# A planned GNN layer: transfers with a distant due time wait while the transfer queue has a backlog

## The chip, the core and the metric

The kernel runs on one NeuronCore of a Trainium2 chip. A core has a TensorE (PE) for matrix products with a separate weight load (PEld), a VectorE (DVE), a ScalarE (ACT), a GpSimd (POOL) and a SyncE (SP). Each has its own queue of instructions and works through it in order; they meet through semaphores. SP only issues transfers (DMAs) here; GpSimd issues some as well. The metric is device time in microseconds (us) for one execution of the whole program; lower is better.

## The reference

One layer of a graph network on 64 graphs of 256 nodes with 256 channels, in fp32. `h` is the layer-normed input after a ReLU, and the layer adds a gated recurrent unit's output to x:

```python
h = jnp.maximum(_layernorm(x, axis=-1), 0.0)
# _L0_gnn_ref(h, adj): h is called x inside it
xc = jnp.transpose(x, (0, 2, 1))
h = relu(bn1(conv1d(xc, conv1_w)))              # 1 tap
h = bn2(conv1d(h, conv2_w, pad=8))              # 17 taps along the nodes
x_conv = jnp.transpose(relu(h + xc), (0, 2, 1))
s = x @ w_se.T + b_se                           # 3 numbers for each node
A = jnp.exp(-dist(s, s)) * mask                 # mask is the adjacency, 256x256 for each graph
x_nmp = einsum('bnm,bmd->bnd', A, relu(x @ w_msg.T + b_msg))
gi = concatenate([x_conv, x_nmp]) @ w_ih.T + b_ih
gh = x @ w_hh.T + b_hh
r, z = sigmoid(gi_r + gh_r), sigmoid(gi_z + gh_z)
out = x + (1 - z) * tanh(gi_n + r * gh_n) + z * x
```

Here `dist` is the squared distance of the two nodes' `s`, and the last line is cut down: inside the layer x means h, and the outer addition uses the layer's own input.

## The kernel before

**Work and loops.** Graphs are handled in pairs (i = 0 to 31) and four pairs make a block of eight graphs; there are eight blocks, called b0 to b7 here (the loop `for b in range(NB)`, line 1237). Inside a block, `nxt` is the first pair of the next one, so each block also prepares the next.

**The 17-tap convolution** is done in 16 frequency bins. `forward` splits the rows into the bins' operands U, V, PT and Sv on VectorE; `product` (line 879) multiplies a bin's operand with that bin's filter spectrum, in four 128x128 matmuls (eight rows in the trace, since an fp32 matmul leaves two). The text counts a block's 47 products as P1 to P47. The spectra lie in DRAM (`filt`): each is a 256 KB load by SP into one of nine slots `wb` (`load_kinds`, line 854). A product gives its slot back and the next load is issued, so the 47 loads W1 to W47 of a block are spread through its products. Two of the nine slots (tz0, tz1) come free only a few products into a block. `branch_back`, `odd_back`, `q_back`, `p_back` and `join` bring the products back on VectorE.

**The other steps of a block.** `message` (w_msg matmuls), `embed` (two transposes "ident,z" and copies to zT), `affinity` (nine-row matmuls of zT, then exp and the product with the adjacency on ACT and DVE, into e), `aggregate` (e,msg matmuls), `conv1` and `split` for the next block, and `gates`, whose matmuls are combined in seven products for each pair (`seven`).

**Transfers, which is what the change concerns.**
- `load_x` (line 591): x of a pair, two DMAs on SP.
- `turn_h` (763): ACT writes hh, then a DMA transpose on SP, written T:halves<-hh; `sort_h` (774): four DMAs hh<-halves on SP; `join_h` (781): ACT copies to hT.
- `turn_adj` (602): a DMA transpose of the adjacency on SP into `halves`, then halves_d<-halves to DRAM; `load_adj` (609): four DMAs adjh<-halves_d on GpSimd; `join_adj` (619): ACT copies.
- `finish` (1156): a DMA transpose of the output on SP (T:gn<-back), ACT copies to back, then on GpSimd two accumulating loads of x onto back and two writes to out. The finish of a block's last pair is done in the next block.
- In b0, GpSimd also loads the gate weights w_ih and w_hh, 2.3 MB.

**What sets the order.** Every engine call goes through `Recorder.record` (line 332), which makes a Task with a modelled cost and, for a transfer, a `size` in us of the transfer queue's service. All instructions therefore carry line 369, the call made there, in the profile. `plan` (line 383) is a list scheduler. It gives each tensor task a due time `late`, the sum of tensor costs ahead of it in program order, and passes due times back to what a task needs. It then takes, again and again, the engine that can begin soonest, and on it the ready task with the earliest due time:

```python
cand = [(max(free[e], at, lane if T[k].size else 0.0), T[k].late, k, at) for at, k in ready[e]]
if cand:
    now = min(cand)[0]
    best.append((now, min(c[1:] for c in cand if c[0] <= now + 1e-9), e))
```

`self.dma` is the modelled time at which all transfers issued so far are through; `lanes` allows eight in flight for SP (with ACT) and eight for GpSimd. `emit` (line 448) then issues the calls in the planned order; nothing is decided on the chip. There are three plans: a prologue in its written order (`emit(True)`), one for the first forward transform and the filter spectra, and one for all eight blocks.

Of the kernel before, what the change touches and what calls it, by code (L numbers as in the profile page):

```python
# [249 lines left out]
class Recorder:  # L250
# [8 lines left out]

    LANES = 8  # L260
    TURN = 1.9
    LAG = {"tensor": 0.25, "vector": 0.14, "scalar": 0.16, "gpsimd": 0.2, "sync": 0.0}
    OWN = {"tensor": 0.0, "vector": 0.12, "scalar": 0.12, "gpsimd": 0.1, "sync": 0.0}

    def __init__(self, nc):
        self.nc, self.tasks, self.live, self.masks = nc, [], {}, {}
        self.first, self.planned, self.dma = None, 0, 3.0
        self.lanes = [deque([0.0] * self.LANES) for _ in range(2)]
        self.free = dict.fromkeys(self.LAG, 0.0)
        for name in ("tensor", "vector", "scalar", "gpsimd", "sync"):  # L270
# [61 lines left out]
    def record(self, engine, op, args, kw):  # L332
# [7 lines left out]
        if op.startswith("dma"):  # L340
            if "transpose" in op:
                size, cost = 2.5, self.TURN
            elif "accum_op" in kw:
# [33 lines left out]
    def lag(self, u, v):  # L377
        return 0.0 if u.size else (self.OWN if u.engine == v.engine else self.LAG)[u.engine]

# [3 lines left out]
    def plan(self, fixed=False):  # L383

        T, new = self.tasks, range(self.planned, len(self.tasks))
        self.planned = len(T)
        total = 0.0
        for k in new:
            t = T[k]
            for p in t.preds:  # L390
                T[p].succs.append(k)
            if t.engine == "tensor":
                t.late = total
                total += t.cost
        for k in reversed(new):
            t = T[k]
            for s in t.succs:
                t.late = min(t.late, T[s].late - self.lag(t, T[s]) - self.cost(t))
            if t.first is not None:
                t.late = t.first - 1e6  # L400
        ready, free = {e: [] for e in self.LAG}, self.free
        left = {}

        def enable(k):
            at = max((T[p].done + self.lag(T[p], T[k]) for p in T[k].preds), default=0.0)
            ready[T[k].engine].append((at, k))
        for k in new:
            left[k] = sum(p in left for p in T[k].preds)
            if not left[k]:
                enable(k)  # L410
        order = []

        def commit(k, e, at, now):
            t = T[k]
            ready[e].remove((at, k))
            t.begin = now
            free[e] = t.done = now + t.cost
            if t.size:
                if t.cost == self.TURN:
                    free[e] = max(free[e], self.dma + 1.1)  # L420
                self.dma = max(self.dma, now + 1.6) + t.size
                t.done = self.dma + 1.1
                lanes = self.lanes[e == "gpsimd"]
                lanes.popleft()
                lanes.append(t.done)
            order.append(k)
            for s in t.succs:
                left[s] -= 1
                if not left[s]:
                    enable(s)  # L430
        while fixed and len(order) < len(new):
            k = new[len(order)]
            e = T[k].engine
            at = next(at for at, j in ready[e] if j == k)
            commit(k, e, at, max(free[e], at, self.lanes[e == "gpsimd"][0] if T[k].size else 0.0))
        while len(order) < len(new):
            best = []
            for e in ready:
                lane = self.lanes[e == "gpsimd"][0]
                cand = [(max(free[e], at, lane if T[k].size else 0.0), T[k].late, k, at) for at, k in ready[e]]  # L440
                if cand:
                    now = min(cand)[0]
                    best.append((now, min(c[1:] for c in cand if c[0] <= now + 1e-9), e))
            now, (_, k, at), e = min(best)
            commit(k, e, at, now)
        return order
# [972 lines left out]
```

## Time and profile before

| | |
|---|---|
| median of 10 runs | 1771.15 us (1763.25 to 1778.35) |
| profiled execution | 1774.74 us, its span 1773.0 us |
| TensorE busy | 1694.2 us (96%) |
| VectorE, ScalarE, GpSimd busy | 1465.9, 1035.6, 300.9 us |
| mean granted TensorE clock | 0.987 |
| share of the DMA engines busy, b2 to b6 | 0.61 to 0.68 in each block |
| first product of b0 to b7 | 109.8, 324.4, 531.85, 738.1, 948.5, 1152.7, 1360.6, 1565.9 us |

How to read it: busy times are of one profiled execution, and its span is the time from its first to its last instruction. In a timeline a row is a run of like instructions: the start in us, its length, the engine, the line, the operation, output and inputs by tile name, and how many; in brackets, how long the engine sat idle before it and who ended that. In the list of waits a row gives the waiting engine and tile, what ended the wait, and then us in total, how often, and the longest. "128x128" is partitions by elements of the tile.

### The profile page before, as it was taken

Reading aid. Unit: us, or ns where it says so; the run is one execution under the profiler, and the core shown is the slowest. Engines: PE = TensorE matmul, PEld = TensorE weight load, DVE = VectorE, ACT = ScalarE, POOL = GpSimd, SP = SyncE. Lnnn points to the kernel's source line nnn. Section 1 sums busy time; section 2 is a strip of 40 time slices with the busy share of each in tenths; the row PEclk is TensorE's granted clock in tenths of the full one; section 3 lists DMA queues with packets and bytes.
Section 4 is the critical chain, followed back from the end, with each engine's and each line's share of the span. In section 5 each row is a group of like instructions: output and inputs, shape, how many; then the busy total and the mean of one; then the engine's idle time right before and its main releaser. Section 6 shows DMA issues by size and latency. Waiting matters only on the chain.

```text
span 1773.0 us, 26175 instructions
## 1 busy us (share of the span) xinstructions
PE 1694.2 (96%) x8950; PEld 1427.4 (81%) x8950; DVE 1465.9 (83%) x3400; ACT 1035.6 (58%) x1949; POOL 300.9 (17%) x353
## 2 busy tenths in 40 slices
PE   5999999999999999899999999999999999999996
PEld 3678788888789778797888887897788978888885
DVE  4889798698897988878987988979888889869543
ACT  2554656665755756556665757557665666556443
POOL 2210222103210221102211132102211022110010
PEclk9999999999999999999999999999999999999998
DMA  7775565973569465693658835694656936383122
GB/s 189 238 242 169 107 131 120 214 207 84 114 133 280 110 126 112 172 250 84 120 119 217 199 90 114 135 272 118 126 112 176 252 78 119 74 232 130 18 55 48
DMA packets 319992, 260.94 MB, mean 147 GB/s; under 512 B 209096, under 2 KB 242148, under 8 KB 319859
## 3 DMA queue, kind: packets, MB, share of 16 engines
q1 hardware_dynamic: 278506, 199.04, 45.4%
q0 software_dynamic: 38400, 57.58, 15.6%
q10 hardware_dynamic: 2953, 2.66, 0.8%
q8 instruction: 70, 1.15, 0.3%
q14 instruction: 63, 0.52, 0.1%
HBM read 156.03 MB, written 43.78 MB: 113 GB/s over the span
## 4 chain that ended last, share of the span: by engine, by line
PE 76%; DVE 9%; ACT 4%; DMA 4%; issue 2%; POOL 2%; ACTq 0%; DVEq 0%; POOLq 0%
PE acc L369 51%; PE aux L369 25%; DMA wb<-filt 4%; DVE V L369 2%; DVE T L369 2%; DVE Yv L369 2%; ACT adj L369 1%; POOL rstd L369 1%; POOL shift L369 1%; DVE U L369 0%; DVE e L369 0%; ACT Yv L369 0%; DMA x<-in_x_dram 0%; ACT hh L369 0%; DVE acc L369 0%
## 5 line engine op out<-in xcount | busy, mean ns | idle before, releaser
L369 PE MATMUL acc<-wb,w_ih 128*128 128x256 f32 x768 | 192.4, 379 | 0.0
L369 PEld LDWEIGHTS acc<-wb,w_ih 128*128 128x128 f32 x768 | 145.9, 190 | 19.8
L369 POOL DMA_DIRECT2D adjh<-halves_d x112 | 66.6, 600 | 531.6 <-ACT adj L369 445.4
L369 PE MATMUL acc<-wb,w_x 128*128 128x256 f32 x576 | 138.0, 384 | 8.3 <-DVE acc L369 8.3
L369 PE MATMUL aux<-wb,w_x 128*128 128x256 f32 x576 | 141.5, 384 | 1.5 <-DVE wb L369 0.9
L369 DVE SCALAR_TENSOR_TENSOR V<-T,V 128x128 f32<-128x128 f32 (+2 forms) x448 | 140.8, 376 | 0.0
L369 PEld LDWEIGHTS acc<-wb,w_x 128*128 128x128 f32 x576 | 108.5, 191 | 35.9 <-DVE acc L369 14.1
L369 POOL TENSOR_TENSOR rstd<-rstd,neg_half 128x4 f32<-128x4 f32 x32 | 86.8, 2714 | 279.3 <-DVE shift L369 252.7
L369 PEld LDWEIGHTS aux<-wb,w_x 128*128 128x128 f32 x576 | 107.3, 191 | 22.1 <-DVE wb L369 3.7
L369 PE MATMUL aux<-w_msg,hT 128*128 128x259 f32 x512 | 124.4, 383 | 0.4 <-ACT fo L369 0.4
L369 PE MATMUL acc<-V,wb 128*128 128x128 f32 x1024 | 121.4, 276 | 1.4 <-DMA wb<-filt 1.3
L369 PEld LDWEIGHTS acc<-V,wb 128*128 128x128 f32 x1024 | 118.8, 192 | 4.0 <-DMA wb<-filt 1.8
L369 POOL DMA_DIRECT2D back<-in_x_dram x62 | 61.5, 1151 | 346.1 <-ACT back L369 346.1
L369 PEld LDWEIGHTS acc<-U,wb 128*128 128x128 f32 x1024 | 119.0, 195 | 1.3 <-issue 0.3
L369 PE MATMUL acc<-U,wb 128*128 128x128 f32 x1024 | 119.4, 278 | 0.0
L369 PE MATMUL acc<-hT,w_hh 128*128 128x256 f32 x384 | 106.2, 385 | 6.9 <-ACT acc L369 6.9
L369 PE MATMUL acc<-Yv,w_ih 128*128 128x256 f32 x384 | 110.6, 384 | 0.9 <-ACT Yv L369 0.8
L369 PE MATMUL aux<-hT,w_c 128*128 128x512 f32 x224 | 107.4, 596 | 3.7 <-ACT e L369 2.7
L369 ACT COPY back<-gn 128x1024 uint16<-128x1024 uint16 x62 | 79.7, 1338 | 53.2 <-DMA gn<-back 53.2
L369 ACT ACTIVATE gn<-acc,bn_columns 128x512 f32<-128x512 f32 x64 | 44.0, 687 | 113.4 <-PE acc L369 110.4
L369 PE MATMUL acc<-wb,w_hh 128*128 128x256 f32 x384 | 109.4, 380 | 0.0
L369 PE MATMUL aux<-e,msg 128*128 128x256 f32 x448 | 109.1, 381 | 0.0
(177 smaller groups left out, 3943.5 us busy)
## 6 DMA issues: line engine op xcount, KB each, us to landing
wb<-filt SPq DMA_DIRECT2D x376, 256.0 KB
back<-in_x_dram POOLq DMA_DIRECT2D x62, 256.0 KB, 7.6
out_dram<-back POOLq DMA_DIRECT2D x62, 256.0 KB, 4.3
x<-in_x_dram SPq DMA_DIRECT2D x58, 256.0 KB
halves_d<-halves SPq DMA_DIRECT2D x28, 512.0 KB
adjh<-halves_d POOLq DMA_DIRECT2D x112, 128.0 KB, 3.1
hh<-halves SPq DMA_DIRECT2D x108, 128.0 KB
filt<-fo POOLq DMA_DIRECT2D x18, 252.0 KB, 5.7
```

The source lines that it names most:

```text
L369: self.tasks.append(Task(engine, lambda: method(*args, **kw), cost, size, self.first))
```

## The change

`plan` gets a notion of how far TensorE's work has come in due times: `self.pace` is the largest `late` of the tensor tasks planned so far. A transfer whose own `late` is more than CALM = 20 us beyond that, and finite, isn't a candidate before `self.dma - 1.0`, that is until the modelled transfer queue is within 1 us of being empty. The candidate's time is now worked out by `when`. Transfers without a due time (the output's) and the fixed prologue are as before. All three plans are made with the new code.

```diff
     TURN = 1.9
+    CALM = 20.0
...
         order = []
+        self.pace = 0.0
+
+        def when(e, at, t):
+            now = max(free[e], at)
+            if t.size:
+                now = max(now, self.lanes[e == "gpsimd"][0])
+                if self.pace + self.CALM < t.late < math.inf:
+                    now = max(now, self.dma - 1.0)
+            return now
 
         def commit(k, e, at, now):
             t = T[k]
             ready[e].remove((at, k))
             t.begin = now
             free[e] = t.done = now + t.cost
+            if e == "tensor":
+                self.pace = max(self.pace, t.late)
             if t.size:
...
             for e in ready:
-                lane = self.lanes[e == "gpsimd"][0]
-                cand = [(max(free[e], at, lane if T[k].size else 0.0), T[k].late, k, at) for at, k in ready[e]]
+                cand = [(when(e, at, T[k]), T[k].late, k, at) for at, k in ready[e]]
```

## Prediction

> **What bounds the kernel now.** I read the page first: busy shares, then the chain that ended last.
>
> ```profile
> PE 1694.2 (96%) x8950; PEld 1427.4 (81%) x8950; DVE 1465.9 (83%) x3400; ACT 1035.6 (58%) x1949; POOL 300.9 (17%) x353
> ...
> PE 76%; DVE 9%; ACT 4%; DMA 4%; issue 2%; POOL 2%; ACTq 0%; DVEq 0%; POOLq 0%
> ```
>
> TensorE sets the end. Its idle time is 1773.0 − 1694.2 = 78.8 us, and a change of order can win only from this, or from time in which the PE runs slow. TensorE's waits say whose it is:
>
> ```profile
> PE aux L369 <- DMA bn_rows<-in_bn_v_dram: 15.5, 1, 15.5
> PE acc L369 <- DMA wb<-filt: 10.4, 12, 2.4
> PE acc L369 <- DVE acc L369: 8.3, 10, 1.9
> PE acc L369 <- ACT acc L369: 6.9, 7, 1.1
> ...
> PE aux L369 <- ACT zT L369: 4.3, 7, 1.6
> ```
>
> The first, before the loops, isn't touched. The second is what the rule can reach: 10.4 us in which a product waits for its filter. I placed each in TensorE's timeline. Three (0.64, 1.44, 2.38 us, 4.5 together) are the first products of b2, b3 and b6; most of the rest (5.9 us) falls on the 15th to 22nd product of a block, where the block's four 128 KB adjh transfers run beside the filter stream. That place in b4:
>
> ```profile
> 961.97 0.60 PE L369 MATMUL aux<-e,msg 128*128 128x256 f32 x2
> 962.93 1.16 PE L369 MATMUL acc<-Sv,wb 128*128 128x128 f32 x8 [0.37 <-DMA wb<-filt]
> 963.93 1.06 PE L369 MATMUL acc<-V,wb 128*128 128x128 f32 x8
> 964.82 1.03 PE L369 MATMUL aux<-e,msg 128*128 128x256 f32 x4
> ```
>
> A product is eight rows, 0.9 us. The planner puts aggregation matmuls (e,msg) and message matmuls (w_msg) between P15 and P24; they cover most of the lateness, and 0.37 us shows. Last, b6's start, in SP's, GpSimd's and TensorE's timelines:
>
> ```profile
> 1335.18 0.38 SPq L369 DMA_DIRECT2D halves_d<-halves  x1
> 1335.73 3.36 SPq L369 DMA_TRANSPOSE gn<-back  x1
> 1354.15 7.92 SPq L369 DMA_DIRECT2D wb<-filt  x8
> ```
> ```profile
> 1353.48 0.63 POOL L369 DMA_DIRECT2D out_dram<-back  x1 [2.55 <-DMA back<-in_x_dram]
> ```
> ```profile
> 1360.60 3.81 PE L369 MATMUL acc<-Sv,wb 128*128 128x128 f32 x32 [2.38 <-DMA wb<-filt]
> ```
>
> The block's last output write runs into W1, the block's first filter load: W1 lands 5.6 us after issue, and 2.8 us in b4, where that write was issued 2.9 us ahead of it and not 0.7.
>
> **What the Trainium skill says.** "DMA: Bandwidth & Descriptors", section "Issuing engines are not separate DMA queues": transfers issued by SP, ACT and GpSimd share the same 16 engines and interleave. The trace agrees: W17 of b4 took 4.9 us from issue to landing, W18 to W21, beside GpSimd's adjh, 5.9 to 7.5. So withholding SP's x or transposes doesn't remove the adjh burst. The same page, "Rules for kernel authors", row "Use all 16 engines": an outer dimension under 16 confines a transfer to that many engines. The trace agrees for x (outermost 8): 256 KB take about 2.0 us of the queue, a filter load of that size 0.67. "TensorE: Matmul & The Clock Gate", Part 1: after an idle window of about 3.4 us the clock is halved. The trace agrees: after a 1.57 us wait in b1 the clock records show half speed from 355.9 to 362.7 and the U products are stretched (8.50 us for 56 rows, 7.31 for 64 in b4).
>
> ```profile
> 354.53 2.86 PE L369 MATMUL aux<-zT 9*128 9x256 f32 x8 [1.57 <-ACT zT L369]
> 357.32 1.23 PE L369 MATMUL aux<-w_msg,hT 128*128 128x259 f32 x2
> 358.34 8.50 PE L369 MATMUL acc<-U,wb 128*128 128x128 f32 x56
> ```
>
> **The change part by part.** No instruction is added or removed; every engine gets the same ones in another order from b0 on. In b2 to b6, SP's order was W1–21, x, W22–24, T:halves<-hh, W25–33, hh, W34–35, hh, W36–41, two hh, T:gn, W42–47. It becomes W1–33, T:halves<-hh, W34–41, three hh, W42–47, hh, T:gn, then adjacency transpose and two x. TensorE's order, planned on these imagined landings, becomes P1–P24 without a break, eight e,msg matmuls together, P25–32, eight w_msg together, P33–40, then both ident,z transposes and four zT matmuls in one group.
>
> (a) *SP before W22.* One x (2.0 us of service) and one transpose (about 1.8 of service, SP held 7.7 us) leave the stream's first half. It matters only from W22 on: W16 to W21 were issued ahead of x in both kernels. Gain for P22–P24 about 2 us of landing.
>
> (b) *TensorE P16–P24 unfilled.* I replay b4 with its own landings: P(k) starts at the later of P(k−1)'s end and its filter. P16 is ready at 961.97 and needs W18 (W11 and W14 fill late slots, for P22 and P23), landed 962.89: 0.9 us. P18 and P19 wait 0.7 each for W20 and W21 (965.42, 967.00). With (a), P24 ends near 972.4; then 8 e,msg at 0.43 = 3.46 us, and the four w_msg matmuls already done by this point before, 1.73: 977.6, against 975.85 where P25 begins now: +1.75. The same for b2, b3, b5, b6: +1.4, −1.0 (its 2.23 us stall at P17 is part of the old time), +1.4, +1.9. If the burst is longer than before this grows one for one, since nothing is left to fill.
>
> (c) *zT merged.* The nine-row zT groups cost about 0.3 us of pipe entry each and a wait of 0.39 in b4; in one group, later: −0.6 a block. (b)+(c) for b2–b6: 0.8 − 1.6 + 1.2 + 0.9 + 1.4 = **+2.7**.
>
> (d) *b1.* The zT group moves behind P44, so the 1.57 us wait and the half-speed spell (products at twice 111 ns: about 3.8 us) go; its P1–P24 stretch costs +2 as in (b): **−3.3**.
>
> (e) *b7.* P1–P24 costs +1.3, but the planner moves T:gn from W21 to W41 and P24's followers start earlier; at 1627–1639 TensorE waits 0.62, 0.49 and 0.92 for DVE and ACT, then runs at half clock for about 6.8 us (3.4 lost), 5.4 in all. I take 60% of it as won: −3.3. **−2.0**, both ends +1.3 and −4.1.
>
> (f) *Block starts.* T:gn of the last finish is now ahead of halves_d. Before it waited for the adjacency transpose to land (1335.05 in b6) though ACT had written back by 1334.5, and shared the engines with halves_d (3.28 us); so it lands 1 to 3 us sooner, and the two back accumulations and the two output writes with it. W1's issue is tied to the last gate's slots and stays. Of the 4.5 us at block starts I take **−3.0**; bounds 0 and −6.2 (all of it, and 1.7 for the half-speed spell, 738.2 to 741.6, behind b3's). halves_d, now behind T:gn, is 3 to 4 us later; its adjh readers wait in a 25 us gap of GpSimd.
>
> (g) *b0.* W10–47 run without a break, but GpSimd puts one rstd power ahead of w_ih and w_hh (2.3 MB, 5.9 us of service at 0.67 us per 256 KB), so they start near 117 and not 110.3, beside W18 onward: 0 to +4 for P16–P24. DVE, the bound later in b0 (waits of 0.80, 0.73, 1.87 and 0.85 between 176 and 204), meets weight_sums (10 us) later: −2 to +3. I take **0**, bounds −2 and +6.
>
> (h) *Hidden moves.* hh×4, T:gn and x end up to 8 us later; the hT they feed is read near 1008 in b4 and landed near 994, x is needed near 1028. At least 6 us remain, so nothing; without that cover the price is the excess, one for one. GpSimd's shift power is now ahead of the first adjh: 0.2 us, inside the burst already priced. The T:halves<-hh behind W33 holds SP up to 7.7 us; the 3.46 us of w_msg behind P32 and seven full slots (7 × 0.9 = 6.3) cover it: nothing, at worst 1 us a block.
>
> Sum: 2.7 − 3.3 − 2.0 − 3.0 + 0 = −5.6. The profiled execution took 1774.74 us, span 1773.0 and 1.7 around it, 3.6 over the median of 1771.15; −5.6 on it gives a span of 1767.4, and on the median **1765.5**.
>
> **The rivals.**
>
> *Faster (0.45):* the sum, 1757 to 1765.8. Its support is the stalls with clock loss at 354 and 1627, which the new orders break up.
>
> *No change (0.28), about 1769.5:* stalls move rather than go. The transfers are hidden anyway, as b4's single 0.37 us stall suggests; (f) yields nothing because the out write still meets W1, and (d) only: 2.7 − 3.3 − 2.0 + 1 = −1.6.
>
> *Slower (0.27), about 1781:* P16–P24 unfilled. Its waits come as runs of 0.7 to 1 us over two or three products. In the trace waits of 1.44, 1.57 and 2.23 us were each followed by a half-speed spell, which costs 1.7 us for each 3.4 us of it; one of 2.38 was not. With the upper replay (+1.9) and that loss in five blocks: 5 × 3.6 = 18, −0.6 × 5 for zT, less (d)+(f) at half (−3), −2: about +10. It decides from roughly 1.4 us of idle in 3.4 us; b4's replay has 2.3 us over about 5 us, so it is near. Against it: b6 had 1.19 us at one product and no slow spell.
>
> **How the numbers follow.** Forecast 1765.5. Repeated runs scatter by 0.4% each way, and about 0.3% (5.3 us) is what a measurement can tell. Range 1755 to 1779: below it (e), (f) and (g) would all be at their best ends; above it lie the slower case's upper third. The likeliest case's own range is 1757 to 1765.8. Faster 0.45, same 0.28, slower 0.27.
>
> **What would show it.** Right: waits for wb still about 8 to 12 us, but in runs at P16–P21 and none at b3's and b6's first products; zT in b1 under 0.5 us and full clock at 355–363; fewer waits at 1627–1639. Wrong: slow-clock spells some 15 us into the blocks (slower), wb waits under 3 us in sum (the rule frees more than I think), b0's first product of b1 later than 324.4 by over 3 us (w_ih), or a long T:halves hold behind W33.

## The result, and the profile after

The changed kernel takes 1760.33 us (median of 14 runs, 1753.08 to 1768.03) against 1771.19 for the kernel before (49 runs). The ratio is 0.9938, 95% interval 0.9923 to 0.9953: 11 us faster. The forecast was 1765.5, with a range of 1755 to 1779 and 0.45 on faster. The profiled execution took 1753.68 us, its span is 1751.9; it is 6.7 below its median, and that of before was 3.6 above its own. The pair of profiles therefore shows 21 us where the runs show 11, so the sizes of stages below are taken over several profiles.

One sentence on the change has to be put right: most output transfers do have a due time, through the reuse of `back` by the next pair's gates. Only the last pair's have none. The rule reaches them too.

Busy shares and chain of the changed kernel (its instructions carry line 370, those of the experiments mostly 373):

```profile
PE 1669.7 (95%) x8950; PEld 1415.1 (81%) x8950; DVE 1463.5 (84%) x3400; ACT 1036.2 (59%) x1949; POOL 308.5 (18%) x353
...
PE 81%; DVE 7%; DMA 6%; ACT 2%; issue 2%; POOL 1%; SPq 0%; ACTq 0%; DVEq 0%
```

TensorE is still the bound. Its idle time has not shrunk (1751.9 − 1669.7 = 82.2 us, 78.8 before); its busy time has, by 24.5 us, with the same 8950 matmuls. So the gain is not in a smaller total of waits. TensorE's waits of the changed kernel agree:

```profile
PE acc L370 <- DMA wb<-filt: 13.0, 20, 1.5
PE acc L370 <- ACT acc L370: 10.3, 7, 1.7
...
PE aux L370 <- ACT zT L370: 2.1, 3, 0.8
```

The waits for filters grew from 10.4 us in 12 to 13.0 in 20, but the longest fell from 2.4 to 1.5; those for ACT's acc grew from 6.9 to 10.3; those for zT fell from 4.3 to 2.1. Busy time can fall in two ways. First, matmuls can run at half clock for less time: between the prologue and the last 20 us the clock records of before hold seven 3.41 us windows at half speed, those of after two (129.1 and 340.7 us), and a window costs about 1.7 us, half its length. That belongs to this pair of executions and not to the change: six profiles of kernels with the rule in b2 to b6, without the fillers of the experiments below, hold one to seven such windows (3.7 on average), the four with the old order two to seven (3.75). Five windows are 8.5 us, most of what the pair of profiles shows beyond the runs. Second, TensorE can spend less time on the nine-row zT groups, which counts as busy; that comes below.

P1 to P25 of b5, TensorE's timeline, changed kernel:

```profile
1139.33 3.81 PE L370 MATMUL acc<-Sv,wb 128*128 128x128 f32 x32 [0.54 <-ACT e L370]
1142.98 7.31 PE L370 MATMUL acc<-V,wb 128*128 128x128 f32 x64
1150.13 3.78 PE L370 MATMUL acc<-Sv,wb 128*128 128x128 f32 x32
1154.72 1.13 PE L370 MATMUL acc<-V,wb 128*128 128x128 f32 x8 [0.82 <-DMA wb<-filt]
1156.80 6.52 PE L370 MATMUL acc<-V,wb 128*128 128x128 f32 x56 [0.94 <-DMA wb<-filt]
1163.15 3.62 PE L370 MATMUL aux<-e,msg 128*128 128x256 f32 x16
```

It is the picture of the forecast's step (b): P1 to P24 bare, two waits beside the adjh burst, P24 finished 23.8 us after P1 (forecast 23.9), then e,msg in one piece. P1 waits 0.54 us for ACT, as it did in this block before. At the start of b6, where P1 waited 2.38 us for its filter, the same 0.54 us is now all that is left. The end of b5 shows why, in SP's, GpSimd's and TensorE's timelines:

```profile
1317.84 1.77 SPq L370 DMA_TRANSPOSE gn<-back  x1
1319.77 1.05 SPq L370 DMA_DIRECT2D halves_d<-halves  x1
1338.34 6.97 SPq L370 DMA_DIRECT2D wb<-filt  x9
```
```profile
1333.61 0.63 POOL L370 DMA_DIRECT2D out_dram<-back  x1 [1.44 <-DMA back<-in_x_dram]
```
```profile
1342.94 3.25 PE L370 MATMUL acc<-Sv,wb 128*128 128x128 f32 x27 [0.54 <-ACT e L370]
```

The last output write is issued 4.7 us ahead of W1, not 0.7.

Times from one block's first product to the next one's (b7: to the start of TensorE's last instruction), from five profiles; the edits of the last two are described below:

| block | before | changed | changed, again | before + tail swap | changed + hh behind acc |
|---|---|---|---|---|---|
| b0 | 214.7 | 213.1 | 216.8 | 213.7 | 212.1 |
| b1 | 207.4 | 205.2 | 206.4 | 207.4 | 203.9 |
| b2 | 206.3 | 203.8 | 205.7 | 206.7 | 203.3 |
| b3 | 210.4 | 203.8 | 204.2 | 205.8 | 202.9 |
| b4 | 204.2 | 203.5 | 204.1 | 206.8 | 202.8 |
| b5 | 207.9 | 203.6 | 208.4 | 205.4 | 203.5 |
| b6 | 205.3 | 204.2 | 204.2 | 205.0 | 202.7 |
| b7 | 199.7 | 197.4 | 201.2 | 197.1 | 196.9 |

b4, on which the forecast was worked out, is the best of the steady blocks of before: the others spread up to 6 us above it.

### The profile page after: what moved, and what is told of

Its sections match the earlier page's. It is cut to its first block, busy times and chain, and to the rows that moved or that the text cites. A ratio compares the mean times of both kernels' runs of the same rounds, so it can differ in the third digit from the quotient of the medians.

```text
span 1751.9 us, 26185 instructions
## 1 busy us (share of the span) xinstructions
PE 1669.7 (95%) x8950; PEld 1415.1 (81%) x8950; DVE 1463.5 (84%) x3400; ACT 1036.2 (59%) x1949; POOL 308.5 (18%) x353
## 3 DMA queue, kind: packets, MB, share of 16 engines
q8 instruction: 70, 1.15, 0.3%
## 4 chain that ended last, share of the span: by engine, by line
PE 81%; DVE 7%; DMA 6%; ACT 2%; issue 2%; POOL 1%; SPq 0%; ACTq 0%; DVEq 0%
PE acc L370 55%; PE aux L370 26%; DMA wb<-filt 4%; DVE V L370 2%; DVE T L370 1%; DVE e L370 1%; DVE acc L370 1%; DMA x<-in_x_dram 1%; DVE U L370 1%; DMA T<-in_x_dram 1%; POOL shift L370 1%; DVE st L370 0%; DMA halves<-hh 0%; DVE tr L370 0%; ACT gn L370 0%
## 5 line engine op out<-in xcount | busy, mean ns | idle before, releaser
L370 POOL TENSOR_TENSOR rstd<-rstd,neg_half 128x4 f32<-128x4 f32 x32 | 91.7, 2867 | 285.0 <-DVE shift L370 257.0
L370 PE MATMUL acc<-hT,w_hh 128*128 128x256 f32 x384 | 105.6, 382 | 10.3 <-ACT acc L370 10.3
L370 DVE TENSOR_TENSOR T<-Yv 128x512 f32<-128x512 f32 (+1 forms) x80 | 42.5, 581 | 87.0 <-ACT Yv L370 86.4
L370 PEld LDWEIGHTS aux<-w_msg,hT 128*128 128x128 f32 x512 | 96.3, 190 | 15.1 <-ACT fo L370 0.8
L370 DVE TENSOR_TENSOR acc<-acc,wb 128x512 f32<-128x512 f32 x64 | 44.2, 691 | 72.2 <-PE acc L370 71.6
```

The lines of the kernel that those rows point to most:

```text
L370: self.tasks.append(Task(engine, lambda: method(*args, **kw), cost, size, self.first))
```

## The experiments

**Early and late half.** The rule is switched by how far TensorE's due times have come; b2 begins at 397 us of them. The early half holds in b0 and b1 only, the late half from b2 on; SP's orders are in each block exactly those of one kernel or the other.

```diff
-                if self.pace + self.CALM < t.late < math.inf:
+                if self.pace + self.CALM < t.late < math.inf and self.pace < 395.0:     # early; late: >= 395.0
```

> The rule applies in b0 and b1 only; from b2 on the orders are those of the kernel before. Theory of the forecast (parts d and g): b1 loses its 1.57 us wait for zT and the half-speed spell behind it, b0 gains nothing: about -3 us, ratio 0.998. Rival 'steady blocks': everything comes from b2 to b7, ratio 1.000 (within 0.001). Rival 'b0 and b1 hold most of it': below 0.996.

> The complement: the rule applies from b2 on only, b0 and b1 are those of the kernel before. Theory of the forecast: about -2.3 us (+2.7 for b2 to b6, -3.0 at block starts, -2.0 in b7), ratio 0.9987. Rival 'steady blocks': -8 to -11 us, ratio 0.994 to 0.9955.

Measured: early 1768.38 us, ratio 0.9972 (0.9955 to 0.9989); late 1759.42 (five runs), ratio 0.9919 (0.9900 to 0.9938), the kernel before beside them 1773.56. The early half is as forecast. The late half is not −2.3 us but some −14 (interval −11 to −18), so the steady blocks hold most of the gain. The two add to some −19 us, more than the −11 of the whole; only the ends of the intervals meet. Whether the late half alone is better than the whole is therefore open.

**The tail swap alone.** From here on a kernel makes both plans, with and without the rule, and edits one engine's order before it is issued.

```diff
 # SP, ends of b0 to b5, orders of the kernel before
  T:halves<-in_adj
- halves_d<-halves
  T:gn<-back
+ halves_d<-halves
  W1 ...
```

> The kernel before with one edit: at the ends of b0 to b5 the last T:gn<-back is issued ahead of halves_d<-halves instead of behind it. Theory of the block starts (part f): the waits of the first products for wb in b2, b3 and b6 go, and with them the half-speed spell behind b3's: -3 to -6 us, ratio 0.9965 to 0.998. Rival 'the products' own order wins': no change, ratio 0.9995 to 1.0005.

Measured: 1766.22 us, ratio 0.9962 (0.9944 to 0.9979). TensorE at the start of b6 in this kernel:

```profile
1354.58 3.59 PE L373 MATMUL acc<-Sv,wb 128*128 128x128 f32 x30 [0.54 <-ACT e L373]
```

No first product waits for wb any more in b2 to b6; out write to W1 is 3.5 to 4.2 us. Only the steps of part (f) were edited and they gave what it said: the transpose of b6's start lands 4.3 us after issue (5.1 before) and the output follows. In the profiles b2 to b6 fall from 1034.1 us in sum to 1029.7. The 6.7 us of the ratio are above the forecast's −3. The half-speed windows behind the waits, which I had as a bound, may belong to it: b3's start has one in the profile of before, b3's and b6's have one each in that of the early half, and no block start has one here.

**The tail swapped back in the changed kernel.**

```diff
 # SP, ends of b1 to b5, orders of the changed kernel
  T:halves<-in_adj
- T:gn<-back
  halves_d<-halves
+ T:gn<-back
  W1 ...
```

> The changed kernel with halves_d<-halves put ahead of the last T:gn<-back again at the ends of b1 to b5. Theory of the block starts, as the edit on the kernel before showed (0.9962): waits for wb come back at the first products of some blocks, and half-speed spells behind them: 3 to 7 us slower than the changed kernel, ratio to it 1.002 to 1.004. Rival 'the new order ahead of it already keeps the output writes clear of W1': equal within 1 us.

Measured: 1760.15 us, ratio 0.9936 (0.9911 to 0.9961), the changed kernel beside it 0.9948: equal within the intervals, the rival was right. The out write is still 3.5 to 5 us ahead of W1 and no first product waits. So the swap is enough to clear the block starts but not needed. In the changed kernel the adjacency transpose ahead of it is issued earlier as well: 26 us ahead of b6's W1 in this run, against 23.5 in the kernel before. The result of (f) held, its single cause did not.

**The changed kernel again**, the yardstick for the runs measured beside it:

> The changed kernel again, as the yardstick of the three runs beside it: ratio 0.992 to 0.995. If the late half alone (rule from b2 on, 0.9919) is the better one, this is slower than that by 2 us or more; if the two halves simply add, this is 0.989 to 0.992.

Measured: 1760.99 us, ratio 0.9948 (0.9929 to 0.9966). Its profile is of a long execution (1769.76 us) and shows one reason why executions differ; it is read below.

**Fillers put back.** First TensorE's order of P1 to P40 as a whole, then only the eight e,msg matmuls, then these with ScalarE's order mended:

```diff
 # TensorE, b2 to b6, orders of the changed kernel
- P1-P24, e,msg x8, P25-P32, w_msg x8, P33-P40
+ P1-P15, e,msg, P16, P17, e,msg x2, P18, e,msg x4, P19, e,msg, P20-P32, w_msg x8, P33-P40
 # first run: the w_msg, too, where the kernel before has them
 # third run, ScalarE as well
- V<-acc x2, Yv, msg, Yv, z x4, msg, Yv, hT<-hh, V<-acc x2
+ V<-acc x2, msg, z x4, msg, V<-acc x2, Yv, Yv, Yv, hT<-hh
```

> The changed kernel with TensorE's order of P1 to P40 in b2 to b6 put back to that of the kernel before (e,msg and w_msg matmuls between P15 and P32), all else changed. Theory of the forecast (part b): the unfilled P16 to P24 cost 1 to 1.5 us a block, so this is 5 to 7 us faster than the changed kernel: about 1754, ratio to before 0.990. Rival 'grouping is what wins' (each mix of shapes costs, and the fillers wait for e): slower than the changed kernel by 3 to 8 us, about 1763 to 1768. Rival 'only the zT group of P41 to P47 counts': equal to the changed kernel within 2 us.

> The changed kernel with the eight e,msg matmuls of b2 to b6 put back among P15 to P24, where the kernel before had them; w_msg stays behind P32, so ScalarE's copy V<-acc keeps the order that it was planned for. Theory of the forecast (part b): the gaps behind late filters are filled, about 1 us a block: 5 us faster than the changed kernel, ratio to it 0.997. Rival 'the e,msg matmuls only take the place of the wait at another product': equal within 1 us. Rival 'grouping is what wins': slower by 3 us or more.

> As the run with the eight e,msg matmuls back among P15 to P24, and in ScalarE's order the second pair of V<-acc copies ahead of the Yv activations that wait for DVE, as the kernel before has it. Theory 'only ScalarE's order made filling slow': the 2.4 to 3.4 us waits for V go and the fillers' gain of 1.2 us a block shows: 4 to 7 us faster than the changed kernel, ratio to before 0.990 to 0.992. Rival 'an early P24 is itself worth it, since DVE's way back of some 11 us starts there': a wait turns up later in the block, equal to the changed kernel or slower.

Measured: 1777.78 us, ratio 1.0018 (1.0002 to 1.0034); 1773.54, 1.0007 (0.9991 to 1.0023); 1772.77, 1.0018 (1.0003 to 1.0033). All three lose the whole gain. The theory of the forecast fell, but half of it is visible: P1 to P25, e,msg included, takes 26.4 and 26.2 us a block in the second and third run against 27.3 in the changed kernel, so the fillers do fill. The time is lost later. TensorE of b3, second run, then third run:

```profile
781.43 2.05 PE L373 MATMUL acc<-U,wb 128*128 128x128 f32 x16 [2.45 <-ACT V L373]
```
```profile
777.66 2.05 PE L373 MATMUL acc<-U,wb 128*128 128x128 f32 x16 [0.74 <-ACT V L373]
...
781.95 5.46 PE L373 MATMUL acc<-PT,wb 128*128 128x128 f32 x32 [2.02 <-ACT acc L373]
```

ScalarE of the second run at this place says what comes in between:

```profile
770.21 1.07 ACT L373 COPY V<-acc 128x512 f32<-128x512 f32 x2 [3.00 <-PE acc L373]
775.65 0.63 ACT L373 ACTIVATE Yv<-Yv 128x512 f32<-128x512 f32 x1 [4.36 <-DVE Yv L373]
...
780.33 1.04 ACT L373 COPY V<-acc 128x512 f32<-128x512 f32 x2
```

P24's result goes through VectorE's way back (a chain of 14 us in the changed kernel, 552.8 to 567.1) to ScalarE's Yv, and the copies that free TensorE's accumulators stand behind those in ScalarE's queue. A filler ahead of P24 makes P24 late; the same filler behind P24 covers VectorE. Mending one place of ScalarE's order moved the wait to the next (from V to acc, 2.0 us). So with the changed kernel's orders of ScalarE and VectorE, bare P1 to P24 are not a plain cost of 1 us a block: it is paid to start a longer chain earlier.

That holds for these orders and not for fillers as such. In the kernel before, whose orders were planned together with the fillers, P24 begins 25.6 us or more into b2 to b6 (25 to 27 in the three filled runs, 23 in the changed kernel), and TensorE has no wait for V or acc between P25 and P47. ScalarE's copies stand ahead of Yv there, in b4:

```profile
988.57 1.07 ACT L369 COPY V<-acc 128x512 f32<-128x512 f32 x2 [1.60 <-PE acc L369]
989.53 1.16 ACT L369 ACTIVATE Yv<-Yv 128x512 f32<-128x512 f32 x2
```

The three runs put one engine's old order beside the new order of others; no run plans fillers and merged zT groups together.

**The zT group split.**

```diff
 # TensorE, b2 to b6, orders of the changed kernel
- P41-P44, zT x4, P45-P47
+ P41, zT x2, P42-P44, zT x2, P45-P47
```

> The changed kernel with the first two of the four zT matmuls moved up behind P41 in b2 to b6, as the kernel before had them. Theory 'the zT group was under-priced in part c': each block loses about 1.5 to 1.9 us again (a wait for zT and a second entry into the nine-row shape), so 8 to 9 us slower than the changed kernel, ratio to it 1.005. The forecast's own price: 0.6 a block, 3 us, 1.0017.

Measured: 1760.42 us, ratio 0.9931 (0.9909 to 0.9953): the time of the changed kernel, and neither forecast. Yet the price is there in the timeline. Split (b3), and then whole (b2 of the changed kernel):

```profile
782.66 1.25 PE L373 MATMUL aux<-zT 9*128 9x256 f32 x4 [0.35 <-ACT zT L373]
783.85 2.94 PE L373 MATMUL acc<-PT,wb 128*128 128x128 f32 x24
786.72 0.70 PE L373 MATMUL aux<-zT 9*128 9x256 f32 x4
787.35 2.83 PE L373 MATMUL acc<-PT,wb 128*128 128x128 f32 x23
```
```profile
577.10 0.71 PE L370 MATMUL aux<-zT 9*128 9x256 f32 x8
577.74 2.94 PE L370 MATMUL acc<-PT,wb 128*128 128x128 f32 x24
```

From its start to the next row's, a group of four rows takes 0.63 us and one of eight 0.64; one of two takes 0.62 in the kernel before. The single rows of a group show why: they begin in two sets some 0.3 us apart, 6 to 7 ns from one row to the next within a set, so the rows of a set run side by side and more of them add nothing. A group right behind a wait takes longer, 1.19 us here. Before had seven zT groups a block, 5.56 us; the change has four, 3.69 (each to the next row's start, waits behind them included but for the one ahead of the next P1). The split kernel pays its fifth group in the products (54.7 us from P1 to P47 against 52.4) and gets most of it back in the gates: the wait of 1.67 us for ACT's acc, which the changed kernel has once a block, is gone in four of the five blocks. TensorE comes later to a place that is timed by others. So the price of a group is read from timelines here; that merging groups shortens the run is not shown by a run of its own.

**That wait.** ScalarE of the changed kernel, b2, and TensorE behind it:

```profile
609.83 0.68 ACT L370 ACTIVATE wb<-acc,b_rz 128x512 f32<-128x512 f32 x1
613.21 1.09 ACT L370 ACTIVATE hh<-x,shift,rstd 128x256 f32<-128x256 f32 x2 [2.71 <-POOL shift L370]
...
615.84 0.58 ACT L370 ACTIVATE acc<-acc 128x512 f32<-128x512 f32 x1
```
```profile
616.48 0.70 PE L370 MATMUL acc<-hT,w_hh 128*128 128x256 f32 x2 [1.67 <-ACT acc L370]
```

The hh activations of the next pair stand ahead of work that TensorE needs, and wait for GpSimd's layer-norm power. I moved them behind it in five blocks:

```diff
 # ScalarE, orders of the changed kernel
- tr, wb, hh, hh, tr, wb, hh, acc<-acc
+ tr, wb, tr, wb, acc<-acc, hh, hh, hh
```

> The changed kernel with one edit of ScalarE's order in five blocks: the first hh activations, which stand ahead of tr, wb and acc<-acc and wait up to 2.7 us for GpSimd's shift, are issued behind acc<-acc. Theory: TensorE's wait of 1.67 us for acc (1.06 in the kernel before) goes, five times, and with it the half-speed spells that it sets off in some executions: 6 to 10 us faster than the changed kernel, ratio to before 0.988 to 0.991. Rival 'the wait is DVE's or TensorE moves into the next wait': within 2 us of the changed kernel.

Measured: 1752.64 us, ratio 0.9900 (0.9875 to 0.9926), 7 to 8 us faster than the changed kernel (0.9938 and 0.9948 in its two sets of runs): the theory held, and this version beats both kernels. ScalarE and TensorE at that place, b3:

```profile
814.64 0.58 ACT L373 ACTIVATE acc<-acc 128x512 f32<-128x512 f32 x1
815.13 1.57 ACT L373 ACTIVATE hh<-x,shift,rstd 128x256 f32<-128x256 f32 x3
```
```profile
816.10 0.59 PE L373 MATMUL acc<-hT,w_hh 128*128 128x256 f32 x2
```

With the fillers as well:

> Both edits together. If both theories hold and add: 10 to 16 us faster than the changed kernel, ratio to before 0.985 to 0.988. If only the edit of hh holds: as that run within 2 us.

Measured: 1763.75 us, ratio 0.9968 (0.9956 to 0.9980): the edit of hh gains 9 us there too, the fillers lose theirs again.

**Both hand edits without the rule.** The tail swap and the move of hh, on the orders of the kernel before.

```diff
 # SP and ScalarE, orders of the kernel before
  the tail swap as above
- tr, wb, hh, hh, tr, wb, hh, acc<-acc
+ tr, wb, tr, wb, acc<-acc, hh, hh, hh
```

> The kernel before, without the rule, with two edits by hand: the last T:gn<-back ahead of halves_d at the ends of b0 to b5, and ScalarE's hh activations behind acc<-acc in five blocks. Theory 'both are independent of the rule': the swap's 0.9962 and the five waits of 1.06 us, 5 us or 0.3%: ratio 0.992 to 0.994, the level of the changed kernel. Rival 'the wait for acc is tied to the rule's order': 0.996, as the swap alone. Rival 'the rule's own orders of b1 and of the products are needed': above the changed kernel by 0.2% or more even with both.

Measured: 1769.52 us, ratio 0.9988 (0.9975 to 1.0000), with the last rival. The wait for ACT is gone and another stands beside it. TensorE, then VectorE, b3:

```profile
832.57 1.56 PE L373 MATMUL acc<-wb,w_x 128*128 128x256 f32 x6 [1.48 <-DVE acc L373]
```
```profile
830.95 0.75 DVE L373 BATCH_NORM_STATS2 st<-x 128x6 f32<-128x256 f32 x2 [5.02 <-DMA x<-in_x_dram]
...
831.84 0.68 DVE L373 TENSOR_TENSOR acc<-acc,wb 128x512 f32<-128x512 f32 x1
```

x is loaded into the tile that hh reads, so a later hh makes a later x, and in the old order VectorE's statistics of that x stand ahead of the sum that TensorE needs. In the changed kernel x and its statistics come later anyway. The result also trims the tail swap's own size: hh's move costs about 0.3 us a block there (1.15 to 1.75 for 1.06), so by this run the swap is worth some 4 us rather than the 6.7 of its own run; the intervals allow both.

## Why the prediction was right, and where its sum was not

The forecast was "faster", and the measured time lies in its range, but nearer to its lower end than to its centre. The direction was forecast from (d) and (f), which held. In b2 to b6 away from the block starts, the sum of (b) and (c) had the wrong sign: +2.7 us was forecast, and the profiles show −5 to −7. By its own steps:

- **(d) b1**, −3.3: measured −2.9 (mean of 10 profiles with the rule there, 204.7 us, against 207.6 in 4 without). The 1.57 us wait for zT and the half-speed windows behind it are gone; the profiled execution has one other such window in b1, at 340.7 us.
- **(g) b0**, 0: measured −0.2 on the same profiles (213.8 and 214.0), with a scatter of 5 us. Waits for filters of 0.34 and 1.47 us at 126 and 129 us, which I had expected from w_ih, are there; the waits between 176 and 204 are gone in exchange, but for one of 1.3 us at 206.
- **(f) block starts**, −3.0: the three waits of 4.46 us became three of 0.54 for ACT, −2.8; in time some −4, by the run with both hand edits. Right in effect; the swap of T:gn and halves_d, named as its cause, is sufficient but not necessary.
- **(b) bare P16 to P24**, in sum +5.4 us over five blocks: measured +1.3, or +3 when the later profiles with the same orders are taken in. P24's end was right within 0.5 us on average. What was too small was the comparison: I replayed b4, the best block of before, while P1 to P25 of the others was longer (mean of 15 blocks without the rule 27.2 us, less the four w_msg matmuls of 1.75 us that they already contain; 15 with it 27.5). And the step looked at TensorE's gaps alone. In three runs a late P24 delayed VectorE's way back and cost more than the fillers gained, with the other engines' orders left as they were.
- **(c) zT merged**, −0.6 a block: **the mis-sized term.** I counted one group less and 0.3 us of entry. It is three groups less, −1.87 a block, and a wait of 0.39 less.
- **(h) hidden moves**, 0: in b2 to b6 TensorE waits for hT, x or gn in neither profile. But arriving earlier has its own wait: ACT's acc went from 1.06 to 1.67 us, five times, −0.6 of (c) each, which I had not listed.
- **(e) b7**, −2.0: **not there**, measured +1.3 (199.2 in 10 profiles, 197.9 in 4, with a scatter of 1 to 2 us in each). The half-speed spell near 1630 us that I hoped to remove is in one of four profiles without the rule and in seven of ten with it, which is about the size of the difference; I had taken one execution's spell for a fixed feature of the kernel.

For b2 to b6 the forecast was −0.3; the runs and profiles say −9 to −11 (1033 us in sum without the rule, 1022 with it). About 4 of these are block starts; the rest fits (c), less the longer wait for ACT's acc and what (b) cost. This is a sum of figures from timelines. No run gives TensorE, ScalarE and VectorE their new orders with SP's old one, so whether the transfers had to move for this gain was not tested. The rival "slower" needed repeated half-speed spells in the first half of a block: the changed kernel's profile has one such window in b1 and none in b2 to b7. Its waits for filters there are 0.2 to 1.1 us each, at two to four products of a block.

## What to carry to other kernels

Where one engine is 96% busy, look for time that counts as busy: groups of small odd shapes, and stretches at half clock behind long waits. Before filling a gap on the bounding engine, follow the result of the instruction that the filler delays: a chain on two other engines may begin there, and their orders have to be planned with the filler. And price a change against several blocks and executions, not the best block of one.

## What was not expected of the hardware

- A group of nine-row matmuls between 128-row ones costs 0.62, 0.63 and 0.64 us for 2, 4 and 8 rows. The Trainium skill ("TensorEngine Tiling (Array Packing)", section "Tiling Modes") says that changing the tiling mode drains TensorE. The trace fits that, though it doesn't show a drain as such: the last full row ahead of a group in b4 takes 0.21 us and so does the first one behind it, against 0.11 for its neighbours. The 0.63 itself is not all the price of a change: two full rows of 256 columns take 0.43 us too. What a group saves by holding more rows is that they run side by side.
- The half-speed windows lie on a grid of 3.41 us: in each profile's clock records, all changes of speed are whole multiples of it apart, but for the first and last entry. The grid lies differently against the kernel's work in each execution. Of 6630 full-speed windows of it in fourteen profiles (the first 100 and the last 20 us left out; matmul ends are modelled, so idle time is approximate), all 29 in which TensorE was idle for more than 1.80 us were followed by half speed; of 48 with 1.4 to 1.8 us, seven were, and of 6553 with less, twelve, eight of them in b7. So the length of a wait doesn't decide, but how much of it falls into one window: in the second profile of the changed kernel TensorE waited 3.36 us in b5 and 3.35 us in b2; the first wait was followed by half speed, the second, which the grid cut into 1.59 and 1.76 us, was not. The prediction read its 1.57 us wait as agreeing with a whole idle window; in these profiles about half a window was enough. Its own limit of 1.4 us was somewhat low.
- GpSimd's power on a 128x4 tile took from 1.03 to 7.43 us in the changed kernel, repeating to 0.01 us at the same place of the steady blocks (1.07, 1.47, 3.28, 7.43). In the second profile the one of 3.28 took 6.41 in b1, b2 and b5. TensorE's wait for acc behind it became 3.36 us in b5 and ended at half clock; GpSimd, then TensorE:

```profile
1226.37 6.41 POOL L370 TENSOR_TENSOR rstd<-rstd,neg_half 128x4 f32<-128x4 f32 x1 [7.13 <-DVE shift L370]
```
```profile
1236.93 1.22 PE L370 MATMUL acc<-hT,w_hh 128*128 128x256 f32 x2 [3.36 <-ACT acc L370]
1237.94 1.06 PE L370 MATMUL acc<-wb,w_hh 128*128 128x256 f32 x2
```

  Two rows of 128x256 take 1.06 us there and 0.59 elsewhere. The skill ("GPSIMD Engine Reference", section "1. Specifications") says that GpSimd shares its memory interfaces with VectorE and contends with instructions that read two inputs. The fourteen profiles agree: of 448 powers the 74 that met no such VectorE instruction took 1.02 to 1.05 us each, and all 148 that took over 3 us lay under such instructions for at least 96% of their time. No run moved VectorE's work away to test it. This and the clock's grid are two ways in which equal programs differ by several microseconds from run to run.
